# Second layer of a graph network on one core: one fp32 product of 48 rows per tile of edges in place of two products of bf16 parts

## The chip, the core and the metric

The kernel runs on one core of a Trainium2 chip. The metric is device time in microseconds (us). A core has a matrix engine (PE, with its weight loads listed as PEld), a vector engine (DVE), a scalar engine (ACT), GpSimd (POOL) and SyncE (SP), which here only starts DMAs. "Median" is over the runs shown; the profile is of one execution.

## The reference

Two layers of a graph network over 12,500 nodes of 64 features and 212,500 edges, sorted by target, one of them a loop on each node. Each layer normalizes, applies relu, passes messages and adds the result to x:

```python
h = relu(layernorm(x))
msg = sum over r of (h[src] * (etypes == r)) @ weight[r]        # 16 relations
x = x + segment_sum(msg, dst)

h = relu(layernorm(x))
m = concat([h[src], h[dst], edge_attr]) @ W1 + b1               # 64 + 64 + 8 rows of W1
msg = relu(m) @ W2 + b2
x = x + segment_sum(msg, dst)
```

## The kernel before

**Tiles.** Edges go in tiles of 128, four tiles to a group (G = 4). The first layer has 1563 tiles in 391 groups (the loops are handled apart), the second 1661 tiles in 416 groups. Nodes lie in 98 blocks of 128. Because edges are sorted by target, the targets of a group fall in a window of W = 40 nodes.

**Order.** Every engine works strictly in written order: a small class (InOrder, L310 to L322) ties each instruction behind the last one of its engine. All records of the trace therefore carry line L319, the helper's, and are told apart by the names of their tiles. What runs beside what is written by hand: each loop over groups issues gathers for group g and, with lags, later steps of earlier groups (L99 and L100: in the second layer z 3 groups later, hid and oh 4, the product pa 6, the sum 9, except near the end).

**First layer** (`first_layer`, L878). For each group POOL gathers 4 x 128 rows of h by an indirect DMA each (`gather`, L658). ACT makes a one-hot over relation and place (off_r, oh_r), PE multiplies it with the gathered rows (pa), DVE adds pa into a table of 16 relations x node. Between those steps generators are advanced one step at a time: `coming` (indices of later edges, loops), `fresh` (start of the next block), `open_step` (`finish(k)`, L697, for a finished pair of blocks) and `beside` (`attributes(chunk)`, L446). `finish` turns the table into x, normalizes, and multiplies with the first two thirds of W1: A (for sources) and B (for targets, with b1). A goes to a_rows in DRAM as fp32. B is split into three bf16 parts that sum to it (bp, L761 to L766) and stored as rows of 3 x 64 in b_rows. `attributes` does the same for the edges' attributes: 26 chunks are loaded (attr_a), split in three bf16 parts by two copies on ACT and two subtractions on DVE, and stored to attr_p in DRAM by three DMAs each. `weights_of_attributes` (L394) splits the last 8 rows of W1 and lays all nine products of parts out as a weight tile w1c_9 of 72 rows.

**Second layer** (`second_layer`, L1007). Four things are added for each edge before the relu: A of the source (gathered), B of the target, the attributes' product and b1 (already in B). For group g:

- SP loads local_bc (every 4 groups: the edges' places in the window, the same on 120 partitions), bw (40 rows of B in three parts, 120 x 64, bf16) and at9 (three parts of 8 attributes, three times over, 72 x 512, bf16). Every 8 groups it reads the windows' first rows into registers.
- POOL gathers rows of a_rows for four tiles. The pool of `rows` has 14 buffers, so the gathers of group g wait until DVE has used those of group g-14.
- ACT makes ohT, the one-hot of the place, from local_bc: off = |place - row| and ohT = relu(1 - off), both 120 x 512.
- PE multiplies, per tile, ohT with bw and at9 with w1c_9, both in bf16, adding in pz.
- Later: DVE z = pz + rows; ACT hid = relu(z); DVE oh, a one-hot of 40 columns; PE pa = hid by oh in fp32 (one tile pa holds four groups); DVE sums += pa. After 17 groups for two blocks, `results` multiplies sums with W2 and b2 (po, fp32) and stores out.

Each fp32 product appears in the trace as two weight loads and two matmuls, each bf16 one as one of each.

Of the kernel before, what the change touches and what calls it, by code (L numbers as in the profile page):

```python
# [37 lines left out]
F32 = mybir.dt.float32  # L38
BF16 = mybir.dt.bfloat16
# [8 lines left out]
P = 128  # L48
N = 12500
D = 64  # L50
# [105 lines left out]
W3 = 3 * W  # L156
A9 = 9 * EA
ACH = 512
# [22 lines left out]
def gnn_kernel(  # L181
# [10 lines left out]
    b_rows = dram.tile([NW, 3 * D], BF16, name="b_rows")  # L192
    attr_p = dram.tile([3, EA, EP], BF16, name="attr_p")
# [32 lines left out]
    neg_w = keep.tile([W3, 1], F32, name="neg_w")  # L226
    G_.iota(neg_w, pattern=[[0, 1]], base=0, channel_multiplier=-1, allow_small_or_imprecise_dtypes=True)
    for k in (2, 1):
        part_k = keep.tile([W3, 1], F32, name=f"part{k}")
        V.tensor_scalar(part_k, neg_w, -float(k * W), float(W), op0=ALU.is_le, op1=ALU.mult)  # L230
        if k == 2:
            part_2 = part_k
    V.tensor_tensor(part_k, part_k, part_2, op=ALU.add)
    V.tensor_tensor(neg_w, neg_w, part_k, op=ALU.add)
# [59 lines left out]
    def in_order():  # L294
        with ExitStack() as c2:
# [83 lines left out]
            w1c = own.tile([EA, D], F32, name="w1c")  # L379
            w1c_p = own.tile([EA, 3, D], BF16, name="w1c_p")  # L380
            w1c_9 = own.tile([A9, D], BF16, name="w1c_9")
# [4 lines left out]
            zero = own.tile([W, 3 * D], BF16, name="zero")  # L386
# [7 lines left out]
            def weights_of_attributes():  # L394
                Q_.dma_start(w1c, w1[2 * D :])
                yield from rest(8)
                for j in range(3):
                    S_.copy(w1c_p[:, j, :], w1c)
                    yield
                    if j < 2:  # L400
                        V_.tensor_tensor(w1c, w1c, w1c_p[:, j, :], op=ALU.subtract)
                    for k in range(3):
                        r = (3 * j + k) * EA
                        Q_.dma_start(w1c_9[r : r + EA, :], w1c_p[:, j, :])
                        yield
# [23 lines left out]
            def locals_of(c):  # L429

                n = NT // NCH
                cs = slice(c * n, (c + 1) * n)
                d = prep.tile([P, n], I32, name="local_e", bufs=1)
                f = prep.tile([P, n // G], I32, name="local_w", bufs=1)
                Q_.dma_start(d, dst_t[:, cs])
                Q_.dma_start(f, first[c * n // G : (c + 1) * n // G].unsqueeze(0).to_broadcast([P, n // G]))
                yield from rest(8)
                V_.tensor_tensor(
                    local[:, cs].rearrange("p (g k) -> p g k", k=G),
                    d.rearrange("p (g k) -> p g k", k=G),  # L440
                    bc(f, 2, G, [P, n // G, G]),
                    op=ALU.subtract,
                )
                yield

            def attributes(c):  # L446

                k = P // EA
                cols = lambda t: t.rearrange("i (k e) -> i k e", k=k)[:, :, c * ACH : (c + 1) * ACH]
                a = wk.tile([P, ACH], F32, name="attr_a")  # L450
                rest = wk.tile([P, ACH], F32, name="attr_r")
                parts = wk.tile([P, 3, ACH], BF16, name="attr_p")
                Q_.dma_start(a, cols(attr_t))
                for _ in range(4):
                    yield
                S_.copy(parts[:, 0, :], a)
                yield
                V_.tensor_tensor(rest, a, parts[:, 0, :], op=ALU.subtract)
                yield
                S_.copy(parts[:, 1, :], rest)  # L460
                yield
                V_.tensor_tensor(parts[:, 2, :], rest, parts[:, 1, :], op=ALU.subtract)
                for j in range(3):
                    Q_.dma_start(cols(attr_p[j]), parts[:, j, :])
                yield
# [231 lines left out]
            def finish(k, psA):  # L697
# [44 lines left out]
                bp = wk.tile([P, BS, 3, D], BF16, name="bp")  # L742
# [12 lines left out]
                for i, pab in enumerate(pabs):  # L755
# [3 lines left out]
                Q_.dma_start(a_rows[rows, :].rearrange("(b p) d -> p b d", p=P), ab[:, 0, :nb, :])  # L759
                yield  # L760
                b_f, bp = ab[:, 1, :nb, :], bp[:, :nb]  # L761
                S_.copy(bp[:, :, 0, :], b_f)
                V_.tensor_tensor(b_f, b_f, bp[:, :, 0, :], op=ALU.subtract)
                yield
                S_.copy(bp[:, :, 1, :], b_f)
                V_.tensor_tensor(bp[:, :, 2, :], b_f, bp[:, :, 1, :], op=ALU.subtract)  # L766
                yield
                Q_.dma_start(
                    b_rows[rows, :].rearrange("(b p) c -> p b c", p=P), bp.rearrange("p b k d -> p b (k d)")
                )  # L770
# [107 lines left out]
            def first_layer(psA, loops_0):  # L878
# [5 lines left out]
                open_step, beside, coming, fresh = iter(()), iter(()), iter(()), iter(())  # L884
# [4 lines left out]
                chunk = 0  # L889
# [28 lines left out]
                for it in range(NGC + L1_ADD[1]):  # L918
                    g = it
                    if g < NGC:  # L920
                        c, kc = part_of(g)
                        if kc == 0:
                            for _ in coming:
                                next(fresh, None)
                            coming = beside_part(c, psA)
                        if g % 12 == 6 and chunk < EP // (P // EA) // ACH:
                            for _ in beside:
                                pass
                            beside = attributes(chunk)
                            chunk += 1  # L930
                        if g % 56 == 16 and g // 56 < NB // LB:
                            load_x(g // 56 * LB, Q_)
                        rows_of[g], n_of[g] = gather(h_rows[:, :], src_c, g, NTC)
# [19 lines left out]
                    for j in range(max(len(now), len(adds))):  # L953
                        for i in range(G):
# [10 lines left out]
                            if i % 2:  # L965
                                next(beside, None)
# [11 lines left out]
                for _ in coming:  # L978
                    pass
                for _ in beside:  # L980
                    pass
# [25 lines left out]
            def second_layer(ps):  # L1007
# [7 lines left out]
                for it in range(NGR + L2_ADD[1]):  # L1015

                    g = it
                    if g < NGR:
                        if g % RG == 0:
                            at_b.update(enumerate(windows(first_row, g, PAD_DST, Q_), g))  # L1020
                        if g % RB == 0:
                            local_bc = wk2.tile([W3, RB * G * P], BF16, name="local_bc", bufs=3)
                            Q_.dma_start(
                                local_bc,
                                dst_l[g : g + RB, :].rearrange("g e -> (g e)").unsqueeze(0).to_broadcast([W3, RB * G * P]),
                            )
                        a_of[g], n_of[g] = gather(a_rows[:, :], src_i, g, NTR)
                        n = n_of[g]
                        if n:
                            bw = wk2.tile([W3, D], BF16, name="bw", bufs=10)  # L1030
                            Q_.dma_start(
                                bw, b_rows[bass.ds(at_b.pop(g), W), :].rearrange("n (k d) -> k n d", k=3)
                            )
                            at9 = wk2.tile([A9, G * P], BF16, name="at9", bufs=10)
                            Q_.dma_start(
                                at9,
                                attr_p[:, :, g * G * P : (g + 1) * G * P]
                                .rearrange("k i e -> (k i) e")
                                .unsqueeze(0)
                                .to_broadcast([3, 3 * EA, G * P]),  # L1040
                            )
                            off = wk2.tile([W3, G * P], BF16, name="off")
                            ohT = wk2.tile([W3, G * P], BF16, name="ohT", bufs=6)
                            S_.activation(
                                off, local_bc[:, (g % RB) * G * P : (g % RB + 1) * G * P], AF.Abs, bias=neg_w
                            )
                            S_.activation(ohT, off, AF.Relu, bias=1.0, scale=-1.0)
                            if g % 2 == 0:
                                pz = ps.tile([P, 2, G, D], F32, name="pz", bufs=4)
                            pz_of[g] = pz[:, g % 2]  # L1050
                            for i in range(n):
                                cols = slice(i * P, (i + 1) * P)
                                T_.matmul(pz_of[g][:, i, :], lhsT=ohT[:, cols], rhs=bw, start=True, stop=False)
                                T_.matmul(pz_of[g][:, i, :], lhsT=at9[:, cols], rhs=w1c_9, start=False, stop=True)
# [531 lines left out]
```

## Time and profile before

| | |
|---|---|
| median of 16 runs | 5314.17 us (5305.53 to 5321.98) |
| profiled execution: time / span | 5307.29 / 5305.4 us |
| granted TensorE clock | 0.521 |
| second layer, from the first gather of a_rows | 2698.8 us to the end |
| busy in 2699 to 5305 us | PE 782, PEld 666, DVE 334, ACT 656, POOL 1571 us |
| DMA share in 62 to 2698 / 2699 to 5305 us | 0.18 / 0.24 |
| POOL gathers, first / second layer | 1485.8 / 1571.1 us busy |

The profile counts as busy only real work; issue of DMAs and semaphore instructions do not count. A row of a group of instructions gives engine, operation, out<-in with partitions x elements, how many, then busy us and mean ns of one, then the idle time just before them and what ended it. "issue" is idle time in which nothing that the profile shows was waited for; "remote" is a release that it cannot name. What each engine did over the span, in fortieths (tenths busy):

```
PE   0434555445544455455532333323323223223323
DVE  4232333223332233223311111111111111111111
ACT  3333444234432344344422222222222222222223
POOL 5645655656546565666545665665665665665663
```

The chain that ended last names little here: 42% of it is put down to "another core or an unknown queue" and 12% to issue.

### The profile page before, as it was taken

To read this page: it belongs to the slowest core of one execution; us is meant where nothing else is said; L and a number is where in the kernel's file an instruction comes from. 1 tells how busy PE (TensorE), PEld (TensorE's weight loads), DVE (VectorE), ACT (ScalarE), POOL (GpSimd) and SP (SyncE) were. 2 spreads that over 40 slices of the span, in tenths; PEclk is the share of its full clock that TensorE was granted. 3 is DMA by queue.
4 is the path that set the end of the run, shared out by engine and by line. 5 is a ranking of instruction groups with operands and counts; after the bars stand their busy time and mean duration, and the time that the engine had idled before them with its cause. 6 is when DMAs were issued, how large, how long until landed. Compare 5 with 4: busy or idle time off the path is not lost.

```text
span 5305.4 us, 52007 instructions
## 1 busy us (share of the span) xinstructions
PE 2073.9 (39%) x15332; PEld 1644.7 (31%) x15332; DVE 1170.2 (22%) x4728; ACT 1710.3 (32%) x3702; POOL 3090.1 (58%) x3279
## 2 busy tenths in 40 slices
PE   0434555445544455455532333323323223223323
PEld 0323444234432344343422222222222222222223
DVE  4232333223332233223311111111111111111111
ACT  3333444234432344344422222222222222222223
POOL 5645655656546565666545665665665665665663
PEclk8555555555555555555555555555555555555555
DMA  3111211111111111111112222222222222222221
GB/s 87 44 34 36 60 40 42 40 36 43 44 38 33 39 43 44 36 32 35 27 47 52 61 56 55 61 56 55 60 56 58 57 56 58 58 56 58 58 54 45
DMA packets 301339, 258.85 MB, mean 49 GB/s; under 512 B 180555, under 2 KB 229102, under 8 KB 300942
## 3 DMA queue, kind: packets, MB, share of 16 engines
q0 software_dynamic: 104576, 107.97, 10.7%
q1 hardware_dynamic: 183173, 144.27, 9.9%
q10 hardware_dynamic: 13298, 3.20, 0.3%
q8 instruction: 124, 2.03, 0.2%
q14 instruction: 168, 1.38, 0.1%
HBM read 228.35 MB, written 26.82 MB: 48 GB/s over the span
## 4 chain that ended last, share of the span: by engine, by line
another core or an unknown queue 42%; issue 12%; PE 7%; DVE 5%; ACT 4%; POOL 3%; DVEq 1%; DMA 0%; SPq 0%; ACTq 0%; POOLq 0%
PE pa L319 3%; POOL rows L319 3%; PE pT L319 2%; ACT off_r L319 2%; DVE oh L319 1%; DVE z L319 1%; DVE table L319 1%; DVE sums L319 1%; PE pz L319 1%; DVEq L319 1%; ACT off L319 0%; ACT oh_r L319 0%; ACT hid L319 0%; ACT ohT L319 0%
## 5 line engine op out<-in xcount | busy, mean ns | idle before, releaser
L319 POOL DMA_INDIRECT rows<-a_rows,src_i x1661 | 1571.1, 946 | 1052.1 <-DVE oh L319 498.9
L319 POOL DMA_INDIRECT rows<-h_rows,src_c x1563 | 1485.8, 951 | 793.1 <-issue 411.3
L319 PE MATMUL pa<-oh_r,rows 128*64 128x96 f32 x6252 | 799.2, 367 | 970.1 <-issue 734.9
L319 PE MATMUL pa<-oh,hid 128*65 128x40 f32 x3322 | 511.5, 296 | 1027.4 <-issue 991.4
L319 PEld LDWEIGHTS pa<-oh_r,rows 128*64 128x64 f32 x6252 | 535.9, 210 | 1175.5 <-issue 1066.6
L319 ACT ACTIVATE hid<-z 128x256 f32<-128x256 f32 x416 | 168.3, 405 | 1878.8 <-DVE z L319 1761.1
L319 PEld LDWEIGHTS pa<-oh,hid 128*65 128x65 f32 x3322 | 445.3, 221 | 1052.0 <-issue 1013.2
L319 ACT ACTIVATE off_r<-iota_s,code 128x192 bf16<-128x192 f32 x1563 | 579.0, 442 | 1.9 <-issue 1.9
L319 ACT ACTIVATE oh_r<-off_r 128x768 f32<-128x768 bf16 x391 | 329.4, 842 | 694.5 <-remote 568.2
L319 DVE TENSOR_TENSOR sums<-sums,pa 65x40 f32 x416 | 76.1, 183 | 2011.7 <-remote 1817.1
L319 PE MATMUL pT<-wrel,table 128*128 128x64 f32 x1568 | 435.7, 426 | 149.1 <-issue 140.1
L319 DVE TENSOR_TENSOR table<-table,pa 128x96 f32 x1563 | 395.1, 253 | 398.7 <-remote 262.4
L319 PEld LDWEIGHTS pT<-wrel,table 128*128 128x128 f32 x1568 | 367.9, 321 | 223.2 <-issue 215.6
L319 PE MATMUL pz<-bw,ohT 120*128 120x64 bf16 x1661 | 248.6, 238 | 411.4 <-issue 308.0
L319 PE MATMUL pz<-w1c,at 72*128 72x64 bf16 x1661 | 249.1, 238 | 298.0 <-issue 293.3
L319 PEld LDWEIGHTS <-ohT 120*128 120x128 bf16 x1661 | 181.1, 128 | 476.4 <-issue 354.6
L319 ACT ACTIVATE off<-local_bc,neg_w 120x512 bf16<-120x512 bf16 x416 | 294.2, 707 | 53.4 <-DMA local_bc<-dst_l 24.3
L319 PEld LDWEIGHTS <-at 72*128 72x128 bf16 x1661 | 182.4, 127 | 318.2 <-issue 316.5
L319 ACT ACTIVATE ohT<-off 120x512 bf16<-120x512 bf16 x416 | 261.8, 629 | 13.0
L319 DVE TENSOR_TENSOR z<-pz,rows 128x256 f32<-128x256 f32 x416 | 173.4, 417 | 252.6 <-issue 169.6
L319 DVE SCALAR_TENSOR_TENSOR table<-b_rel,rsel,hT 128x256 f32<-128x256 f32 (+1 forms) x400 | 171.9, 469 | 187.9 <-remote 156.3
L319 POOL DMA_INDIRECT edges_c<-c_out,c_to x16 | 14.7, 920 | 211.0 <-DVE table L319 168.0
(177 smaller groups left out, 1060.6 us busy)
## 6 DMA issues: line engine op xcount, KB each, us to landing
local_bc<-dst_l SPq DMA_DIRECT2D x104, 480.0 KB
at<-attr_p SPq DMA_DIRECT2D x416, 72.0 KB
rows<-a_rows,src_i POOLq DMA_INDIRECT x1661
rows<-h_rows,src_c POOLq DMA_INDIRECT x1563
attr_p<-attr_p SPq DMA_DIRECT2D x78, 128.0 KB
attr_a<-in_attr_t SPq DMA_DIRECT2D x26, 256.0 KB
bw<-b_rows SPq DMA_DIRECT2D x416, 15.0 KB
b_rel<-t_loop SPq DMA_DIRECT2D x48, 128.0 KB
```

The lines of the kernel that those rows point to most:

```text
L319: last_ins[self.engine] = getattr(self.engine, name)(*args, **kw)
```

## The change

- b_rows holds B as fp32, 64 columns; the parts bp and their steps in `finish` are gone, and A and B are stored one behind the other.
- attr_p, `attributes`, its generator `beside` and the parts of the weights are gone. Ten kept tiles b_win (48 x 64, fp32) have the attributes' 8 rows of W1 in rows 40 to 47, loaded once by ten small DMAs; rows 0 to 39 are loaded with B's window for each group, in turn.
- In the second layer a tile of_edges (48 x 2048, fp32, three buffers) serves four groups: ACT writes the one-hot into rows 0 to 39, for two groups at once, and one DMA loads the edges' attributes into rows 40 to 47. local_bc has 40 partitions in place of 120.
- Per tile PE makes one fp32 product of 48 rows in place of bf16 products of 120 and 72 rows.

Instructions in the program, second layer, before and after: SP DMAs 940 and 628, SP semaphore instructions 916 and 409, ACT activations 1249 and 833, ACT semaphore instructions 364 and 422, PE semaphore instructions 239 and 344. First layer: SP DMAs 418 and 314, ACT copies 354 and 203, DVE operations on two tensors 1998 and 1844.

```diff
-    b_rows = dram.tile([NW, 3 * D], BF16, name="b_rows")
-    attr_p = dram.tile([3, EA, EP], BF16, name="attr_p")
+    b_rows = dram.tile([NW, D], F32, name="b_rows")
...
+            b_win = [own.tile([WE, D], F32, name=f"b_win{k}") for k in range(NBW)]
...
             def weights_of_attributes():
...
+                for t in b_win:
+                    Q_.dma_start(t[W:, :], w1[2 * D :])
                     yield
...
-                Q_.dma_start(a_rows[rows, :].rearrange("(b p) d -> p b d", p=P), ab[:, 0, :nb, :])
-                yield
-                b_f, bp = ab[:, 1, :nb, :], bp[:, :nb]
-                S_.copy(bp[:, :, 0, :], b_f)
-                V_.tensor_tensor(b_f, b_f, bp[:, :, 0, :], op=ALU.subtract)
-                yield
-                S_.copy(bp[:, :, 1, :], b_f)
-                V_.tensor_tensor(bp[:, :, 2, :], b_f, bp[:, :, 1, :], op=ALU.subtract)
...
+                for k, to in enumerate((a_rows, b_rows)):
+                    Q_.dma_start(to[rows, :].rearrange("(b p) d -> p b d", p=P), ab[:, k, :nb, :])
+                yield
...
-                            if i % 2:
-                                next(beside, None)
...
-                            local_bc = wk2.tile([W3, RB * G * P], BF16, name="local_bc", bufs=3)
+                            local_bc = wk2.tile([W, RB * G * P], BF16, name="local_bc", bufs=3)
...
+                            of_edges = wk2.tile([WE, RB * G * P], F32, name="of_edges", bufs=3)
+                            Q_.dma_start(of_edges[W:, :], attr_t[:, g * G * P : (g + RB) * G * P])
...
-                            bw = wk2.tile([W3, D], BF16, name="bw", bufs=10)
...
-                            at9 = wk2.tile([A9, G * P], BF16, name="at9", bufs=10)
...
-                            S_.activation(ohT, off, AF.Relu, bias=1.0, scale=-1.0)
+                            bw = b_win[g % NBW]
+                            Q_.dma_start(bw[:W, :], b_rows[bass.ds(at_b.pop(g), W), :])
                             if g % 2 == 0:
+                                cols = slice(g % RB * G * P, (g % RB + 2) * G * P)
+                                off = wk2.tile([W, 2 * G * P], BF16, name="off")
+                                S_.activation(off, local_bc[:, cols], AF.Abs, bias=neg_w)
+                                S_.activation(of_edges[:W, cols], off, AF.Relu, bias=1.0, scale=-1.0)
...
                             for i in range(n):
-                                cols = slice(i * P, (i + 1) * P)
-                                T_.matmul(pz_of[g][:, i, :], lhsT=ohT[:, cols], rhs=bw, start=True, stop=False)
-                                T_.matmul(pz_of[g][:, i, :], lhsT=at9[:, cols], rhs=w1c_9, start=False, stop=True)
+                                k = (g % RB * G + i) * P
+                                T_.matmul(pz_of[g][:, i, :], lhsT=of_edges[:, k : k + P], rhs=bw, start=True, stop=True)
```

More of the change, by code (lines that the diff above doesn't have):

```diff
@@ L155 @@
 LEAST, MOST = bounds()
-W3 = 3 * W
-A9 = 9 * EA
-ACH = 512
+WE = W + EA
+NBW = 10
 RG = 8
@@ L224, in gnn_kernel @@
     G_.iota(iota_s, pattern=[[1, RW]], base=0, channel_multiplier=0, allow_small_or_imprecise_dtypes=True)
-    neg_w = keep.tile([W3, 1], F32, name="neg_w")
+    neg_w = keep.tile([W, 1], F32, name="neg_w")
     G_.iota(neg_w, pattern=[[0, 1]], base=0, channel_multiplier=-1, allow_small_or_imprecise_dtypes=True)
[L228 to L234, printed above, removed]
     def stats(pool, x_b, nb, name):
@@ L377, in in_order @@
             G_.dma_start(w2b[D:DA, :], b2.unsqueeze(0))
-            w1c = own.tile([EA, D], F32, name="w1c")
-            w1c_p = own.tile([EA, 3, D], BF16, name="w1c_p")
-            w1c_9 = own.tile([A9, D], BF16, name="w1c_9")
+            b_win = [own.tile([WE, D], F32, name=f"b_win{k}") for k in range(NBW)]
             NHID = 6
@@ L385, in in_order @@
                 G_.memset(t[:, :, D:], 1.0)
-            zero = own.tile([W, 3 * D], BF16, name="zero")
+            zero = own.tile([W, D], F32, name="zero")
             G_.memset(zero, 0.0)
@@ L394, in weights_of_attributes @@
             def weights_of_attributes():
[L395 to L398, printed above, removed]
+                for t in b_win:
+                    Q_.dma_start(t[W:, :], w1[2 * D :])
                     yield
[L400 to L404, printed above, removed]
-                        yield
             def local_targets():
@@ L443, in locals_of @@
                 )
-                yield
[L446 to L464, printed above, removed]
                 yield
@@ L741, in finish @@
                 ab = wk.tile([P, 2, BS, D], F32, name="ab")
-                bp = wk.tile([P, BS, 3, D], BF16, name="bp")
                 pabs = []
@@ L758, in finish @@
                 rows = slice(b0 * P, (b0 + nb) * P)
-                Q_.dma_start(a_rows[rows, :].rearrange("(b p) d -> p b d", p=P), ab[:, 0, :nb, :])
+                for k, to in enumerate((a_rows, b_rows)):
+                    Q_.dma_start(to[rows, :].rearrange("(b p) d -> p b d", p=P), ab[:, k, :nb, :])
                 yield
-                b_f, bp = ab[:, 1, :nb, :], bp[:, :nb]
-                S_.copy(bp[:, :, 0, :], b_f)
-                V_.tensor_tensor(b_f, b_f, bp[:, :, 0, :], op=ALU.subtract)
-                yield
-                S_.copy(bp[:, :, 1, :], b_f)
-                V_.tensor_tensor(bp[:, :, 2, :], b_f, bp[:, :, 1, :], op=ALU.subtract)
[L767 to L770, printed above, removed]
             codes_of = {}
@@ L883, in first_layer @@
                 first_begin = []
-                open_step, beside, coming, fresh = iter(()), iter(()), iter(()), iter(())
+                open_step, coming, fresh = iter(()), iter(()), iter(())
                 n_of, oh_of, rows_of, pa_of = {}, {}, {}, {}
@@ L888, in first_layer @@
                 of_oh = turns((0, 0), NGC, lambda g: BEGIN + g // 2 if g < 2 * BEGIN else 0)
-                chunk = 0
                 def part_of(g):
@@ L925, in first_layer @@
                             coming = beside_part(c, psA)
[L926 to L930, printed above, removed]
                         if g % 56 == 16 and g // 56 < NB // LB:
@@ L978, in first_layer @@
                 for _ in coming:
-                    pass
-                for _ in beside:
                     pass
@@ L1021, in second_layer @@
                         if g % RB == 0:
-                            local_bc = wk2.tile([W3, RB * G * P], BF16, name="local_bc", bufs=3)
+                            local_bc = wk2.tile([W, RB * G * P], BF16, name="local_bc", bufs=3)
                             Q_.dma_start(
                                 local_bc,
-                                dst_l[g : g + RB, :].rearrange("g e -> (g e)").unsqueeze(0).to_broadcast([W3, RB * G * P]),
+                                dst_l[g : g + RB, :].rearrange("g e -> (g e)").unsqueeze(0).to_broadcast([W, RB * G * P]),
                             )
+                            of_edges = wk2.tile([WE, RB * G * P], F32, name="of_edges", bufs=3)
+                            Q_.dma_start(of_edges[W:, :], attr_t[:, g * G * P : (g + RB) * G * P])
                         a_of[g], n_of[g] = gather(a_rows[:, :], src_i, g, NTR)
@@ L1029, in second_layer @@
                         if n:
-                            bw = wk2.tile([W3, D], BF16, name="bw", bufs=10)
-                            Q_.dma_start(
-                                bw, b_rows[bass.ds(at_b.pop(g), W), :].rearrange("n (k d) -> k n d", k=3)
-                            )
-                            at9 = wk2.tile([A9, G * P], BF16, name="at9", bufs=10)
[L1035 to L1046, printed above, removed]
-                            S_.activation(ohT, off, AF.Relu, bias=1.0, scale=-1.0)
+                            bw = b_win[g % NBW]
+                            Q_.dma_start(bw[:W, :], b_rows[bass.ds(at_b.pop(g), W), :])
                             if g % 2 == 0:
+                                cols = slice(g % RB * G * P, (g % RB + 2) * G * P)
+                                off = wk2.tile([W, 2 * G * P], BF16, name="off")
+                                S_.activation(off, local_bc[:, cols], AF.Abs, bias=neg_w)
+                                S_.activation(of_edges[:W, cols], off, AF.Relu, bias=1.0, scale=-1.0)
                                 pz = ps.tile([P, 2, G, D], F32, name="pz", bufs=4)
```

## The prediction

> **What bounds the kernel now.** I first read busy time and the 40 slices, then the groups of instructions, then the waits, then the timeline of one stretch. All records stand under the helper's line L319, so I go by tiles.
>
> ```profile
> span 5305.4 us, 52007 instructions
> ...
> PE 2073.9 (39%) x15332; PEld 1644.7 (31%) x15332; DVE 1170.2 (22%) x4728; ACT 1710.3 (32%) x3702; POOL 3090.1 (58%) x3279
> ...
> L319 POOL DMA_INDIRECT rows<-a_rows,src_i x1661 | 1571.1, 946 | 1052.1 <-DVE oh L319 498.9
> L319 POOL DMA_INDIRECT rows<-h_rows,src_c x1563 | 1485.8, 951 | 793.1 <-issue 411.3
> ...
> L319 PE MATMUL pz<-bw,ohT 120*128 120x64 bf16 x1661 | 248.6, 238 | 411.4 <-issue 308.0
> L319 PE MATMUL pz<-w1c,at 72*128 72x64 bf16 x1661 | 249.1, 238 | 298.0 <-issue 293.3
> ...
> L319 ACT ACTIVATE off<-local_bc,neg_w 120x512 bf16<-120x512 bf16 x416 | 294.2, 707 | 53.4 <-DMA local_bc<-dst_l 24.3
> L319 ACT ACTIVATE ohT<-off 120x512 bf16<-120x512 bf16 x416 | 261.8, 629 | 13.0
> ```
>
> No engine is full. POOL is the busiest; its two rows of gathers fill the two layers. The second layer runs from the first gather of a_rows, 2698.8 us, to the end: 416 groups in 2606 us, 6.26 us each. A gather takes 0.95 us plus 0.30 us of issue, so four cost 5.0 us; the rest is POOL waiting for DVE (498.9 us). Where, the waits of 3000 to 5000 us show, and the timeline at the end of PE's burst and around the pause after it (start, duration, engine, in brackets the idle time before):
>
> ```profile
> DVE sums L319 <- remote: 1641.8, 76, 22.1
> POOL rows L319 <- DVE oh L319: 403.3, 79, 5.6
> ```
>
> ```profile
> 4011.90 1.08 PE L319 MATMUL pa<-oh,hid 128*65 128x40 f32 x8
> ```
>
> ```profile
> 4027.10 0.94 POOL L319 DMA_INDIRECT rows<-a_rows,src_i  x1 [0.30 <-issue]
> ...
> 4029.04 0.22 PE L319 MATMUL pa<-oh,hid 128*65 128x40 f32 x1 [2.58 <-issue]
> ...
> 4032.03 0.19 DVE L319 TENSOR_TENSOR sums<-sums,pa 65x40 f32 x1 [21.74 <-remote]
> ...
> 4032.93 0.94 POOL L319 DMA_INDIRECT rows<-a_rows,src_i  x1 [4.89 <-DVE oh L319]
> ```
>
> The pattern repeats about every 25 us. POOL issues 16 gathers (20 us), then pauses 4.9 us because no buffer of rows is free (gather g needs z(g-14)). At the start of a run PE, ACT and DVE work at full rate for some 6 us: PE takes 1.58 us per group (ACT's off, ohT and hid end it: 0.71 + 0.63 + 0.40). Then they almost stop: PE and SP issue one instruction per 0.7 us by turns, marked "issue", with nothing waited for. The sum that DVE starts at 4032.03 (group 196) waits, by its semaphore, for the last of the eight matmuls shown, whose group 199 closes the tile pa of four groups; they end at 4012.98, yet the sum starts 19 us later, when POOL has stood still for 4 us. Counting instructions of all engines from one recovery to the next slow-down gives 183 (174 to 194 in 8 of 10), while the time varies from 7.3 to 11.4 us. I read this as an allowance of instructions, not of time, refilled when POOL stops; in the slow part about 2 per us pass. A group holds some 56 instructions, so a cycle carries 183 + 2 x 20 = 223, four groups. **The second layer's period is 5.0 us plus a 4.9 us pause shared by the n = 4 groups of a cycle.**
>
> In the first layer POOL also paces; 12 pauses over 15 us make 398.8 us (first fill and last wait included), in which ACT is busy 311.9 us catching up.
>
> **The change part by part.**
>
> *First layer, ACT and DVE.* Gone are 52 casts of attr_p (15.6 + 15.7 us), 100 of bp (28.8): 60.1 us on ACT. On DVE 36.6 us for the attributes and 28.6 for ab and bp. Most lies beside POOL's gathers and is worth nothing. What counts stands in the long pauses: 6.0 us of attr_p and 8.5 us of bp on ACT, where ACT is busy 78% and ends the catch-up. I take 10 us there, and 2 us in the tail, where the last blocks' bp stand ahead of the last copies and POOL waits 62.1 us for a_rows. Sum **-12 us**; bounds 0 (DVE ends every pause) and -25 (tail and shorter pauses too).
>
> *First layer, SP.* 26 loads and 78 stores of attr_p go, the stores of b_rows no longer wait for casts, 10 small loads replace weights and parts of w1c. SP waits 233.2 us for attr_p by the waits, but its other loads (edges, b_rel) are issued well ahead; taken at 0.
>
> *Second layer, PE.* Per tile two bf16 products (two weight loads, two matmuls) become one fp32 product, which the rows show as two weight loads and two matmuls too: pa has 3322 = 2 x 1661. The instruction count stays, the duration does not. No row has 48 rows by 64 columns in fp32; the nearest is po, with a 65x128 weight and 64 columns:
>
> ```profile
> 4033.12 1.09 PE L319 MATMUL po<-w2b,sums 65*128 65x64 f32 x4
> ```
>
> ```profile
> L319 PE MATMUL po<-w2b,sums 65*128 65x64 f32 x196 | 54.5, 422 | 85.2 <-DVE sums L319 68.9 <-issue 16.3
> ```
>
> Four in 1.09 us, one of them 0.42: a step of (1.09 - 0.42)/3 = 0.223 us. The bf16 steps in the timeline are 0.054 us. Eight pairs per group: 0.43 before, 1.79 after, **+1.36 us per group, 566 us of PE in all**. Bounds per step: 0.11 (the pa row, 40 columns and 65 weights, 8 in 1.08 us) and 0.223; I take po's, as its columns and weights are the same. With pa (0.88) and po a group costs PE 2.77 us, against 5.0 us that POOL needs, so PE stays under POOL if it may issue. What hides it: four groups are 11.1 us in a 25 us cycle. If the cover goes, see the slower rival.
>
> [...]
>
> *Second layer, ACT.* off and ohT of 120x512 per group become 40x1024 per two groups. From the forms 128x192 (442 ns), 128x512 (602) and 128x1024 (the table copy, 1045) I take 1.05 to 1.2 us each, 1.1 to 1.2 us per group where 1.34 stood. ACT alone: 1.6 per group with hid, no bound.
>
> *Second layer, SP and DMA.* 416 loads at (72 KB) become 104 of_edges (64 KB), local_bc shrinks to a third, bw from 15 to 10 KB. The DMA share is 0.24 in this stage, so bytes are worth nothing. The new buffers come free with the same lead: three of_edges of four groups as local_bc before, ten b_win as bw. What queues behind SP's wait for PE's reading of of_edges is only the next group's bw; PE is read to be that far anyway.
>
> *Instructions.* SP loses 819 instructions in layer two, ACT 358, PE gains 105 waits: -2.6 of 56 per group. In addition a slower burst lets more pass at 2 per us: 4 us longer, +8. So a cycle carries (183 + 8 + 40)/53.4 = 4.3 groups instead of 4. But DVE's sums wait for tiles of four groups (pa), so part is lost; with n = 4.2 the period falls by 4.9 x (1/4 - 1/4.2) = 0.058 us, times 416 **-24 us**; bounds 0 (n stays 4) and -40 (n = 4.35). I take -18.
>
> Sum -12 - 18 = **-30 us** on the profiled 5307.3, which stood 6.9 us under the median; on the median of 5314.2 that gives **5284 us** (own range 5250 to 5303).
>
> **Rivals.**
>
> *Slower: the fast stretch is one of time.* If the engines slow down 6 to 7 us after recovery whatever they issued, PE at 2.77 us does 6.5/2.77 = 2.3 groups there and 0.6 in the slow part (20 instructions of 34), 2.9 per cycle. Then 5.0 + 4.9/2.9 = 6.7 us per group, +0.47 to +0.53: +195 to +220 us; with the remainder done inside the pause (1.1 x 2.77 = 3 us in 104 cycles) up to +310. It decides as soon as PE's burst of 11 us exceeds the stretch. Time near **5530**. For it: bursts of one length here come with one count, so count and time are hard to part; against: in the first layer, long runs of POOL slow down after 8 us with some 180 instructions, after 14 us with 212, after 26 with 243. Chance 0.14. A milder form, where the longer PE burst only delays some sums past the slow-down (5325 to 5420): 0.12.
>
> *Much faster.* Those matmuls end barely 0.6 us before the slow-down (4013.6). If DVE's next sum slips in, a cycle can hold eight groups: half the 514 us of pauses goes, 5314 - 250 = **5060**; in between 5060 to 5250. Against: PE's instructions per cycle stay limited. Chance 0.10.
>
> *No change.* n stays 4, and the first layer's pauses are ended by DVE's adds: 5304 to 5324. The change would then not do what it removes work for. Chance 0.16.
>
> **How the numbers follow.** Forecast 0.48, much faster 0.10, same 0.16, slower 0.12 + 0.14. Faster 0.58, same 0.16, slower 0.26; 0.2% (10.6 us) is about what a measurement can tell from no change. Range: 5200 to 5420 leaves out the far slower and most of the much faster case, some 0.2; the unknown step of fp32 lies inside, as it is hidden or falls to the slower rival.
>
> **What would show it.** pz with 3322 matmuls at steps near 0.22 us; POOL's pauses in layer two still near 5 us, some 97 to 100 of them instead of 101; the slow-down after about as many instructions but later; the wait of POOL for DVE in the first layer's long pauses down by some 10 us. The forecast is wrong if pauses grow past 5.5 us, if pauses come after fewer than 16 gathers, or if DVE's z waits for pz.

## The result and the profile after

The changed kernel takes 5182.82 us (median of 8, 5177.44 to 5185.94) against 5314.74 us of before on the same chip: ratio 0.9752, interval 0.9744 to 0.9760, **132 us faster** where 30 were forecast and 5200 was the lower end. The profiled execution has a span of 5179.4 us, 126.0 under that of before.

The page after, in the rows that answer those of before (the helper now stands at L310):

```profile
span 5179.4 us, 50346 instructions
...
PE 2624.6 (51%) x15332; PEld 2206.4 (43%) x15332; DVE 1117.3 (22%) x4570; ACT 1579.4 (30%) x3131; POOL 3077.9 (59%) x3279
...
L310 POOL DMA_INDIRECT rows<-a_rows,src_i x1661 | 1567.0, 943 | 943.9 <-issue 436.9
L310 POOL DMA_INDIRECT rows<-h_rows,src_c x1563 | 1477.8, 945 | 801.2 <-issue 406.0
...
L310 PE MATMUL pz<-b_win,of_edges 48*128 48x64 f32 x3322 | 844.0, 410 | 523.2 <-issue 478.8
...
L310 ACT ACTIVATE off<-local_bc,neg_w 40x1024 bf16<-40x1024 bf16 x208 | 235.8, 1134 | 32.2 <-issue 16.7
...
L310 ACT ACTIVATE of_edges<-off 40x1024 f32<-40x1024 bf16 x208 | 219.8, 1057 | 6.6
```

PE is 551 us busier and the kernel is faster: nearly all of PE's added time is hidden. Cut at POOL's gathers, the span moved like this (us; a pause is a gap of over 0.8 us between two gathers of a_rows):

| | before | after | |
|---|---|---|---|
| start to first gather of a_rows | 2698.8 | 2668.8 | -30.0 |
| first to last gather of a_rows | 2561.0 | 2450.7 | -110.3 |
| of that, pauses: number, sum, median | 101, 513.7, 5.13 | 98, 406.5, 4.11 | -107.2 |
| last gather to the end | 45.6 | 59.9 | +14.3 |
| groups per pause: 1661 tiles / 4 / runs of gathers | 4.07 | 4.19 | |

There are hardly fewer pauses; each is a microsecond shorter. In POOL's waits of 2900 to 5000 us, first of before, then of after, the columns being us in total, times, longest:

```profile
POOL rows L319 <- DVE oh L319: 424.1, 83, 5.6
```

```profile
POOL rows L310 <- DVE oh L310: 342.3, 83, 5.8
```

83 pauses in both, on average 5.11 us each before and 4.12 us after. The timeline of after around one of them:

```profile
4030.43 0.94 POOL L310 DMA_INDIRECT rows<-a_rows,src_i  x1 [0.30 <-issue]
...
4032.44 0.23 PE L310 MATMUL pa<-oh,hid 128*65 128x40 f32 x1 [0.40 <-issue]
...
4034.54 0.23 PE L310 MATMUL pa<-oh,hid 128*65 128x40 f32 x1 [1.18 <-issue]
...
4034.68 0.42 DVE L310 TENSOR_TENSOR z<-pz,rows 128x256 f32<-128x256 f32 x1 [16.46 <-issue]
...
4035.37 0.94 POOL L310 DMA_INDIRECT rows<-a_rows,src_i  x1 [4.00 <-DVE oh L310]
```

PE still crawls at one instruction per 0.7 us until 3.2 us after POOL's last gather (it ends at 4031.37); then everything restarts. DVE's first work comes a median 3.2 us after POOL's last gather (before 4.2), and POOL follows it by 0.7 to 0.9 us. In one of three pauses (33 of 98, before 7 of 101) DVE already stood at z and no longer at the sum, so it had got its sums in ahead of the slow part. The slow part also begins later. Counted from DVE's first work after a pause to the first gap of over 0.6 us between instructions of the engines other than POOL, the fast part lasts a median 11.6 us and 196 instructions, where it was 6.8 us and 172; another choice of the gap moves these numbers, but after stays the longer one. A new step of the product, eight in 1.97 us, is the 0.22 us of the po row:

```profile
4034.70 1.97 PE L310 MATMUL pz<-b_win,of_edges 48*128 48x64 f32 x8
```

### The profile page after: what moved, and what is told of

The parts are those of the page before. It is cut to its first block, busy times and chain, and to the rows that moved or that the text cites. A ratio compares the mean times of both kernels' runs of the same rounds, so it can differ in the third digit from the quotient of the medians.

```text
span 5179.4 us, 50346 instructions
## 1 busy us (share of the span) xinstructions
PE 2624.6 (51%) x15332; PEld 2206.4 (43%) x15332; DVE 1117.3 (22%) x4570; ACT 1579.4 (30%) x3131; POOL 3077.9 (59%) x3279
## 4 chain that ended last, share of the span: by engine, by line
another core or an unknown queue 23%; issue 22%; PE 19%; DVE 4%; ACT 3%; POOL 2%; DVEq 1%; DMA 0%; ACTq 0%; POOLq 0%
PE pa L310 8%; PE pz L310 8%; PE pT L310 3%; POOL rows L310 2%; ACT off_r L310 1%; DVE table L310 1%; DVE z L310 1%; ACT off L310 1%; DVE oh L310 1%; DVE sums L310 1%; PE po L310 0%; ACT oh_r L310 0%; DVEq L310 0%; PE hT L310 0%
## 5 line engine op out<-in xcount | busy, mean ns | idle before, releaser
L310 POOL DMA_INDIRECT rows<-a_rows,src_i x1661 | 1567.0, 943 | 943.9 <-issue 436.9
L310 POOL DMA_INDIRECT rows<-h_rows,src_c x1563 | 1477.8, 945 | 801.2 <-issue 406.0
L310 PE MATMUL pa<-oh_r,rows 128*64 128x96 f32 x6252 | 782.8, 363 | 941.2 <-issue 677.3
L310 PE MATMUL pz<-b_win,of_edges 48*128 48x64 f32 x3322 | 844.0, 410 | 523.2 <-issue 478.8
L310 PEld LDWEIGHTS pz<-b_win,of_edges 48*128 48x128 f32 x3322 | 765.4, 319 | 582.1 <-issue 509.6
L310 PEld LDWEIGHTS pa<-oh_r,rows 128*64 128x64 f32 x6252 | 528.1, 208 | 1126.3 <-issue 991.2
L310 PE MATMUL pa<-oh,hid 128*65 128x40 f32 x3322 | 510.8, 302 | 548.0 <-issue 519.4
L310 ACT ACTIVATE hid<-z 128x256 f32<-128x256 f32 x416 | 159.9, 406 | 1889.2 <-DVE z L310 1522.8
L310 PEld LDWEIGHTS pa<-oh,hid 128*65 128x65 f32 x3322 | 426.7, 220 | 605.2 <-issue 541.8
L310 ACT ACTIVATE off_r<-iota_s,code 128x192 bf16<-128x192 f32 x1563 | 578.7, 442 | 1.9 <-issue 1.9
L310 ACT ACTIVATE oh_r<-off_r 128x768 f32<-128x768 bf16 x391 | 329.3, 842 | 795.7 <-remote 710.7
L310 DVE TENSOR_TENSOR table<-table,pa 128x96 f32 x1563 | 395.3, 253 | 667.7 <-remote 488.9
L310 PE MATMUL pT<-wrel,table 128*128 128x64 f32 x1568 | 433.8, 423 | 170.5 <-issue 158.8
L310 PEld LDWEIGHTS pT<-wrel,table 128*128 128x128 f32 x1568 | 366.5, 318 | 253.6 <-issue 246.9
L310 DVE TENSOR_TENSOR sums<-sums,pa 65x40 f32 x416 | 76.1, 183 | 1321.5 <-remote 1066.5
L310 DVE TENSOR_TENSOR z<-pz,rows 128x256 f32<-128x256 f32 x416 | 174.1, 419 | 817.9 <-issue 664.9
L310 ACT ACTIVATE off<-local_bc,neg_w 40x1024 bf16<-40x1024 bf16 x208 | 235.8, 1134 | 32.2 <-issue 16.7
L310 DVE SCALAR_TENSOR_TENSOR table<-b_rel,rsel,hT 128x256 f32<-128x256 f32 (+1 forms) x400 | 172.1, 469 | 255.5 <-remote 217.9
L310 ACT ACTIVATE of_edges<-off 40x1024 f32<-40x1024 bf16 x208 | 219.8, 1057 | 6.6
L310 DVE TENSOR_TENSOR x_sb<-x_sb,pT 128x128 f32<-128x128 f32 (+1 forms) x50 | 14.2, 284 | 571.4 <-remote 315.5
L310 POOL DMA_INDIRECT edges_c<-c_out,c_to x16 | 14.7, 916 | 199.7 <-DVE table L310 162.9
L310 ACT COPY table<-table 128x1024 f32<-128x1024 f32 x49 | 51.2, 1045 | 263.5 <-DVE table L310 244.5
```

Source lines behind the costliest of these rows:

```text
L310: last_ins[self.engine] = getattr(self.engine, name)(*args, **kw)
```

## The experiments

All on the changed kernel unless said otherwise. "Stalls" are the slow stretches seen above, in which PE and SP pass one instruction per 0.7 us while POOL gathers. The experiments ran on several chips, and this became the main finding: on some, before takes 5307 or 5274 us and shows the stalls; on others the same kernel takes 4147 us and shows none. So times are compared by the ratio to before on the same chip; the columns in us are of one profiled execution each. The runs with stalls:

| run | ratio to before, interval | to first gather | first to last gather | rest | pauses: number, median us |
|---|---|---|---|---|---|
| after | 0.9752 [0.9744, 0.9760] | 2668.8 | 2450.7 | 59.9 | 98, 4.11 |
| e1 attributes' parts back | 0.9779 [0.9762, 0.9795] | 2682.6 | 2448.4 | 60.0 | 95, 4.09 |
| e2 one bf16 product | 0.9652 [0.9631, 0.9673] | 2666.2 | 2415.4 | 40.3 | 73, 4.86 |
| e3 two | 0.9719 [0.9703, 0.9735] | 2669.9 | 2443.6 | 44.6 | 90, 4.17 |
| e4 three | 0.9786 [0.9770, 0.9803] | 2670.0 | 2474.2 | 47.2 | 103, 4.23 |
| e13 SP, ACT, local_bc back | 0.9789 [0.9772, 0.9805] | 2654.0 | 2451.0 | 58.7 | 99, 4.12 |
| e14 ACT per group | 0.9753 [0.9735, 0.9771] | 2653.9 | 2430.8 | 58.9 | 90, 3.93 |
| e15 load of 72 KB back | 0.9786 [0.9769, 0.9802] | 2651.7 | 2447.7 | 63.1 | 96, 4.07 |

e1 to e4 ran where before took 5307.53 us, e13 to e15 where it took 5274.22 us.

**e1: the first layer's attributes, put back.** Their result is not read.

```diff
+                        if g % 12 == 6 and chunk < EP // (P // EA) // ACH:
+                            beside = attributes(chunk)
...
+                            if i % 2:
+                                next(beside, None)
```

> After, with the attributes' split into bf16 parts put back in the first layer as work whose result nobody reads (26 loads, 52 ACT copies, 52 DVE subtractions, 78 stores); the second layer is that of after. Theory: the first layer gave 30 us (first gather of a_rows at 2668.8 in place of 2698.8), and the attributes carry about two thirds of it: first gather at 2685 to 2692, time 5200 to 5206, second layer unchanged within 10 us. Rival (the 30 us come from B's parts bp and the shorter finish): first gather at 2669 to 2675, time 5183 to 5190.

The first gather of a_rows came at 2682.6 us, 13.8 later than in after; the second layer did not move by more than 2.3 us. That lies between the two expectations. So of the first layer's 30 us the attributes hold 14, and 16 are left for B's parts and the shorter `finish`, which were not put back alone. Some of it is the gathers themselves. The groups of h_rows, before (above, 951 ns), after (945) and here:

```profile
L312 POOL DMA_INDIRECT rows<-h_rows,src_c x1563 | 1481.7, 948 | 792.5 <-issue 406.8 <-remote 272.4 <-DMA rows<-h_rows,src_c 32.9
```

From before to after that is 8.0 us of the 30; POOL's pauses of over 15 us make up 28.0 (398.8 to 370.8), and shorter ones took 6 back.

**e2, e3, e4: PE's pace against PE's count.** B and one-hot in bf16, the attributes' product left out (B is rounded to bf16), the product made once, twice or three times. The lines for two:

```diff
-T_.matmul(pz_of[g][:, i, :], lhsT=of_edges[:, k : k + P], rhs=bw, start=True, stop=True)
+T_.matmul(pz_of[g][:, i, :], lhsT=of_edges[:, k : k + P], rhs=bw, start=True, stop=False)
+T_.matmul(pz_of[g][:, i, :], lhsT=of_edges[:, k : k + P], rhs=bw, start=False, stop=True)
```

> After, with the second layer's product in bf16: B and the one-hot in bf16, attributes' rows of the weight at zero (the attributes' product is left out), one bf16 product per tile, so two PE instructions per tile in place of four, some 37 of all engines per group in place of 53, and PE's burst short. Theory of an allowance of instructions: more groups per cycle, n near 6, second layer about 2400 + 50, time near 5100 (5060 to 5140). Theory that the slower fp32 burst itself made the gain (its longer time lets the others catch up): the gain goes back, 5250 to 5300. Theory that PE is hidden and the gain came from DMA bytes: within 10 us of 5183.

> As the bf16 kernel with one product, but each product is made twice, so PE has as many instructions per tile as after (and as before) and the short burst of before. Allowance of instructions, with a trickle per us: 53 per group as after, but a burst that is 1.2 us per group shorter lets less trickle in, so between before and after: 5200 to 5260. Allowance of instructions alone, without the pace: 5183 within 10. Pace theory: 5270 to 5314 less the first layer's 30, so 5240 to 5290. DMA theory: 5183 within 10.

> As the bf16 kernel with each product made three times: 69 instructions per group, PE's burst still shorter than in after. Allowance of instructions: n near 3.2, 5.0 + 4.9/3.2 = 6.5 us per group, time 5380 to 5480. Pace or DMA theory: as the kernel with two products, within 20 us.

Measured 5126.28, 5160.35 and 5194.66 us: e2 as the allowance of instructions had it, e3 and e4 outside of every range written down for them. Eight more PE instructions per group cost 34 us each time, by more pauses (73, 90, 103), not longer ones in e4. The pace theory falls: e3 has the short burst of before and yet keeps the gain. By the ratios it is 0.0033 of before, some 18 us, faster than after; the profiled spans are 21.3 us apart, 15.3 of them in the rest behind the last gather and 7.1 between gathers. So fp32 costs the kernel some 20 us here and brings no shorter pauses. My allowance of a fixed number of instructions falls too: e4 passes 61 instructions per group, more than the 56 of before, still moves four groups per cycle (93 of its 103 pauses come after 16 gathers, before 94 of 101), and pauses 4.2 us. Its POOL waits, 2900 to 5000 us:

```profile
POOL rows L310 <- DVE oh L310: 372.4, 88, 4.6
```

4.23 us each, against 5.11 before. e2's 5.6 groups per pause were near the 6 expected, but with pauses of 4.86 us.

These longer pauses show something that the period "5.0 us plus a pause shared by n groups" leaves out: the pause grows with the run of gathers ahead of it. Medians by the length of the run, where there are at least six:

| gathers in the run | before | after | e2 | e4 |
|---|---|---|---|---|
| 12 | - | 3.60 us (9 pauses) | - | - |
| 16 | 5.13 us (94) | 4.07 us (70) | 3.97 us (7) | 4.23 us (93) |
| 20 | - | 5.42 us (7) | 4.80 us (29) | - |
| 28 | - | 5.69 us (6) | 5.74 us (30) | - |

So a longer cycle saves far less than a fixed pause shared by more groups would: in after the pause costs 1.02 us per group behind 16 gathers (four groups), 1.08 behind 20 and 0.81 behind 28. At the same run of 16, before alone pauses for 5.1 us.

**e5 to e12: single parts put back, on chips without the stalls.** ACT's one-hot per group (e5, e10), a 2 KB load more per group (e6), a 72 KB load more per group (e7, e11), local_bc on 120 partitions (e8), the three together (e12), and after itself (e9). The edits, in this order:

```diff
+                            cols = slice(g % RB * G * P, (g % RB + 1) * G * P)
+                            off = wk2.tile([W, G * P], BF16, name="off")
...
-                                cols = slice(g % RB * G * P, (g % RB + 2) * G * P)
-                                off = wk2.tile([W, 2 * G * P], BF16, name="off")
...
+                            more = wk2.tile([EA, D], F32, name="more", bufs=10)
+                            Q_.dma_start(more, w1[2 * D :])
...
+                            more = wk2.tile([9 * EA, 2 * P], F32, name="more", bufs=10)
+                            Q_.dma_start(
+                                more,
+                                attr_t[:, g * 2 * P : (g + 1) * 2 * P].unsqueeze(0).to_broadcast([9, EA, 2 * P]),
+                            )
...
-                            local_bc = wk2.tile([W, RB * G * P], BF16, name="local_bc", bufs=3)
+                            local_bc = wk2.tile([3 * W, RB * G * P], BF16, name="local_bc", bufs=3)
```

> After, with ACT's one-hot made for one group at a time (off and relu of 40x512, 416 pairs) as before, in place of two groups at a time: +0.86 ACT instructions per group and some 0.2 us per group more ACT time. Allowance of instructions: by the three bf16 kernels 8 PE instructions per group cost 34 us, so 0.9 cost some 4 us: 5180 to 5195. ACT theory (fewer, longer ACT steps brought the shorter pause): 30 to 60 us back, 5215 to 5245. Data theory (the DMAs of SP): 5183 within 6.

> After, with one more load per group on SP, 2 KB from DRAM into a ring of ten tiles that nobody reads: +416 DMAs and their semaphore instructions, hardly any bytes. SP theory (the slow part is shared by turns between PE and SP, so each SP instruction takes a turn from PE): 40 to 90 us back, 5220 to 5275. Data theory (bytes or packets of SP's loads): 5183 within 10. Allowance of instructions: +2 per group, 5187 to 5195.

> As the kernel with one more load per group, but 72 KB per load in 72 rows of 1 KB, as large as the load of at9 before. SP theory: as the 2 KB load within 15 us. Data theory: 40 to 90 us more than the 2 KB load, near 5250. Both at work: more than either.

> After, with local_bc loaded to 120 partitions as before (480 KB every four groups) of which ACT still reads 40; no instruction more. Data theory: 30 to 70 us back, 5215 to 5255. SP, ACT and allowance theories: 5183 within 8.

> The changed kernel itself, on the chip of this set. Where before takes about 5310 us (stalls of PE and SP while POOL gathers): 5183 within 8. Where before takes about 4148 us, as on the chip of the last four kernels, POOL never pauses in the second layer, so neither PE's longer product nor the removed work reaches the end there: both theories give 4135 to 4145, and the gain of the second layer is then shown to exist only with the stalls.

e5 to e8 took 4140.00, 4141.80, 4141.05 and 4141.02 us where before took 4147.84; e9 to e12 took 4140.41, 4139.69, 4141.42 and 4140.52 where before took 4146.15 us. After is 0.9987 of before there (0.9977 to 0.9996), 5.7 us. The expectations of e5 to e8 had not reckoned with such a chip; those of e9 and the rest of its set held. e9's POOL waits of 2100 to 4100 us, its gathers of a_rows and one stretch of its timeline:

```profile
POOL rows L310 <- issue: 423.1, 1388, 0.3
POOL rows L310 <- DMA rows<-a_rows,src_i: 65.2, 214, 0.3
POOL rows L310 <- DVE sums L310: 0.3, 1, 0.3
```

```profile
3000.84 0.94 POOL L310 DMA_INDIRECT rows<-a_rows,src_i  x1 [0.30 <-issue]
3002.09 0.95 POOL L310 DMA_INDIRECT rows<-a_rows,src_i  x1 [0.30 <-issue]
```

No pause in 1661 gathers: 1.25 us each, 2073.1 us from the first to the last, 10.9 us behind it. This is the floor of the second layer, and PE's fp32 product, ACT and SP all fit under it. The first layer stalls too: POOL's pauses of over 15 us there make 44.6 us in e9 and 370.8 in after. The two traces of one and the same kernel differ in one more thing. The trace of e9 holds some 89 semaphore events per group in the second layer. The first load in the trace of after, r_first, ahead of any stall, lands with 16 events (2.63 to 3.03 us from the start), and 16 for each of five and a half DMAs per group give 88. But in the second layer (2900 to 5000 us) the trace of after on the chip with stalls holds 20.3, that of before 16.0. In these two traces most of the records are missing.

So in the traces with stalls the words "issue" and "remote" say little: the event that ended a wait may be one of those that are missing. That PE passes its instructions slowly without a wait of the program's own is seen inside one group: its eight products all need the same two tiles, hid and oh, and the first of them has run. In before:

```profile
4017.60 0.22 PE L319 MATMUL pa<-oh,hid 128*65 128x40 f32 x1 [1.23 <-issue]
...
4018.99 0.22 PE L319 MATMUL pa<-oh,hid 128*65 128x40 f32 x1 [1.17 <-issue]
...
4021.34 0.22 PE L319 MATMUL pa<-oh,hid 128*65 128x40 f32 x1 [2.12 <-issue]
```

Eight of them took 1.08 us for the group before (from 4011.90), and these three alone take 3.96 us.

**e13 to e15: the same parts, on a chip with the stalls.** The edits are those of e12, e5 and e7.

> After, with ACT's one-hot per group, a 72 KB load per group and local_bc on 120 partitions, so that only the fp32 product, the width of the one-hot and the first layer differ from before. On a chip with the stalls, if SP, ACT or data made the second layer's 96 us: 5260 to 5290, pauses back at 5.1 us; if the product or the narrower one-hot made it: 5180 to 5210, pauses at 4.1 us. Without the stalls: 4141 within 3.

> After, with ACT's one-hot per group. On a chip with the stalls: ACT theory 5215 to 5245; allowance of instructions 5180 to 5195; data theory 5183 within 6. Without the stalls: 4140 within 2.

> After, with one more load of 72 KB per group on SP that nobody reads. On a chip with the stalls: SP and data theories 5220 to 5275; allowance of instructions 5187 to 5195. Without the stalls: 4141 within 2.

ACT's larger steps are worth nothing that these runs can tell (0.9753 against 0.9752 for after, e14's interval being some 9 us to either side). SP's load gives back 0.0034, some 18 us, which lies between the two expectations, and local_bc's bytes nothing beyond it. The pauses stay short in e13; its POOL waits of 2900 to 5000 us:

```profile
POOL rows L310 <- DVE oh L310: 343.5, 84, 6.0
```

4.09 us each, with as many instructions per group (55.7) as before (55.9) and 130 of its 144 MB in the queue of SP's DMAs; between the gathers of a_rows it is 91 MB against 87 before. So neither ACT's steps, one more load on SP nor bytes made the pause of before longer. Two things did not come back with e13. Nobody reads its added load, so SP waits for a semaphore 428 times in the second layer, as in after (427), where before waits 936 times. And its queue carries 166 packets per group, more than after's 66 but fewer than before's 230.

**e16 to e18: parts taken from before.** The first bf16 part of B alone in loads and one-hot (e16), in the loads alone (e17), no at9 and no attributes' product (e18).

```diff
-bw = wk2.tile([W3, D], BF16, name="bw", bufs=10)
+bw = wk2.tile([W, D], BF16, name="bw", bufs=10)
...
-T_.matmul(pz_of[g][:, i, :], lhsT=at9[:, cols], rhs=w1c_9, start=False, stop=True)
```

> Before, with the first bf16 part of B alone in the second layer: bw of 40 rows (40 packets in place of 120 per group), local_bc, off and ohT on 40 partitions; at9 and its product stay (the two other parts of B are left out). On a chip with the stalls: if the 120 rows of B's load or of the one-hot make the longer pause, pauses of 4.1 us and 1.5 to 2% under before; if the attributes' loads and second product make it, pauses of 5.1 us and within 0.5% of before. Without the stalls: within 0.2% of before.

> Before, with only the 40 rows of B's first part loaded per group into ten kept tiles of 120 rows (the other 80 rows are zero, so two parts of B are left out); local_bc, off, ohT and the product keep their 120 rows. On a chip with the stalls: if the many small packets of bw (80 of 128 bytes more per group than after) are what counts, as the kernel with one part, pauses near 4.1 us; if the rows of the one-hot count, as before, 5.1 us. Without the stalls: within 0.2% of before.

> Before, without the loads of at9 and the attributes' product in the second layer (it is left out), so one bf16 product of 120 rows per tile and one DMA per group less. On a chip with the stalls: by the bf16 kernels, 8 PE instructions per group less are worth some 34 us; if the attributes' loads (SP waiting for PE twice per group) make the longer pause, 120 to 150 us under before with pauses of 4.1 us or fewer of them; if not, 25 to 60 us under before, pauses at 5 us. Without the stalls: within 0.2% of before.

They ran on a chip without the stalls: 4147.78, 4147.54 and 4147.15 us, before 4147.14 us. All three keep before's first layer, and all three stand at before's time; taking a product and a load per group out of the second layer gains nothing there. The gathers of h_rows in e16 and in e9:

```profile
L312 POOL DMA_INDIRECT rows<-h_rows,src_c x1563 | 1492.8, 955 | 502.2 <-issue 381.0 <-DMA rows<-h_rows,src_c 92.0 <-DVE l_f L312 26.2
```

```profile
L310 POOL DMA_INDIRECT rows<-h_rows,src_c x1563 | 1484.5, 950 | 503.3 <-issue 393.8 <-DMA rows<-h_rows,src_c 79.2 <-DVE l_f L310 27.3
```

8.3 us less, and the first gather of a_rows at 2054.7 in place of 2062.3 us. The two ran on different chips, but e5 and e17 on theirs give the same picture (948 and 954 ns, 2052.1 and 2062.8 us): without the stalls the change is worth its shorter gathers in the first layer, and that is all.

## Why the prediction was wrong

- **The step that failed is the second layer's term**, "a 4.9 us pause shared by the n = 4 groups of a cycle". I moved n and held the pause. n came out as forecast (4.19 for 4.2), and the three pauses fewer are worth 3 x 5.09 = 15 us of the 18 taken. But the pause fell from 5.09 to 4.15 us on average (sums over numbers), 98 x 0.94 = 92 us, which I had not priced, not even as a rival. The gathers gave 3 us more. With the first layer's 30 us and 14 us lost at the end this is the 126 us by which the spans differ.
- That n agrees is in part luck: I had set 4.2 by hand below a computed 4.3, and the allowance behind it fell. The cycles of after are also not the ones I had in mind: 13 of its pauses come after 12 or 4 gathers, which I had named as a sign of being wrong, and 15 after 20 or more.
- *First layer*: -12 forecast, -30.0 measured, over my bound of -25. ACT's and DVE's work in the long pauses was mis-sized: the pauses lost 26 us, not 10, while the last wait for a_rows fell by 1.9 us, as taken. My reading of these pauses was off too: inside them ACT is busy 264 us and DVE 258 of the 398.8, so ACT has 66%, not 78%, and DVE as much. The 8 us by shorter gathers were not thought of.
- *PE's fp32 product*: the term held. +566 us forecast, PE busy in the second layer 782 to 1355 (+573), steps of 0.22 us, hidden under POOL. What I left out is the end: with no gather to hide behind, the last groups take 59.9 in place of 45.6 us, +14.3.
- *ACT*: 1.05 to 1.2 us per step forecast, 1.134 and 1.057 measured; no effect on the time that e14 can tell. The three steps beside the 1.58 us per group add up to 1.74; they overlap.
- *SP*: taken as worth nothing but its instructions; e15 gives 18 us for one load of 72 KB per group.
- *Slower rival (stretch of time)*: fell. The fast part now lasts longer (11.6 for 6.8 us) and ends later in count too.
- *Much faster*: the measured time lies in the 5060 to 5250 us given to this rival, but not by its mechanism, which was half the pauses. There are 98 for 101. DVE does get its sums in earlier in a third of the cycles, but only 7 of the 98 runs of gathers reach seven groups or more.
- *Allowance of instructions*: right as far as the slow part came later, as forecast, and in that fewer PE instructions give fewer pauses (e2 to e4, 34 us per eight). Wrong as a fixed number: the instructions of the second layer, divided by its cycles (one more than its pauses), are 229 per cycle before and 225 after, but 245 in e4 and 255 in e2. Nor is the slow part's rate fixed: by the count above it passes a median 1.7 instructions per us beside POOL's before, 1.9 after and 2.7 in e4.
- **What stays open**: why before restarts 4.2 us after POOL's last gather and every other kernel, behind 16 gathers, after 3.0 to 3.3. What separates them is before's 120 rows of B and one-hot and the attributes' second load and product, with the second wait of SP per group and the smaller packets that come with them. e16 to e18 were made to tell these apart and ran where nothing stalls, so it wasn't settled. The 92 us are thus located in the pause, and their cause is not shown.
- What causes the stalls is open as well. In the trace of after with the stalls fewer records arrive than without (20.3 against some 89 events per group); whether the one has to do with the other no run shows.

## What to carry to other kernels

When all engines wait for "issue" at a fixed step and the trace lacks semaphore events, compare the number of events with what the program must make (16 per DMA here), and run the kernel on another chip before explaining the time: here one change was worth 2.5% with the stalls and 0.13% without. A pause was a chain of its own here (last gather, first work of DVE a median 3.2 us later, release of POOL): price its parts, and see whether it grows with the run ahead of it, not only how often it comes. Work that was hidden in the steady state showed behind the last transfer here, with 14 us.

## What the runs showed of the hardware

- The same kernel took 5314, 5307 and 5274 us on chips with the stalls and 4146 to 4148 us on three without; gathers back to back took 1.25 us each on both (0.95 and 0.30 to the next), and PE's granted clock was 0.51 to 0.53.
- With the stalls, POOL's pause behind a run of gathers grew with the run: 3.6, 4.1, 5.4 and 5.7 us behind 12, 16, 20 and 28 gathers in after.
- An fp32 product with a 48x128 weight steps at 0.22 us per pair of load and matmul, like one with 65 rows (0.223): between these two the number of rows does not show. In bf16 it steps at 0.054 us there (e4: twelve in 0.82 us, one of them 0.23).
- An indirect gather of 128 rows of 256 bytes got 5 ns shorter (0.951 to 0.945, and 0.955 to 0.950 us without stalls) when ACT, DVE and SP did less beside it; which of them does it was not tried alone.
